# Four relations' count tables loaded as two plain halves and joined on VectorE

## The chip, the cores and the metric

The kernel runs on one core of one Trainium2 chip. The metric is device time in microseconds (us) of one execution; less is better. All arithmetic is in float32.

## The reference, cut to what matters

A graph network with two parts over the same 384 nodes: an attention layer (L0) and a two-layer relational convolution (L1) with 6 relations and 4 basis matrices. Only L1's use of the edge counts bears on the change:

```python
# one R-GCN convolution; n = 384 nodes, R = 6 relations, B = 4 bases, D = 768
W = jnp.einsum('rb,bio->rio', comp, basis)
h_all = jnp.einsum('ni,rio->rno', x, W)
counts = jnp.zeros((R, n), x.dtype).at[edge_type, dst].add(1.0)
norm = 1.0 / counts[edge_type, dst]
msg = h_all[edge_type, src] * norm[:, None]
agg = jax.ops.segment_sum(msg, dst, num_segments=n)
return agg + x @ root + bias
```

The sum over 12672 edges equals, for each relation r, a 384 x 384 matrix of edge counts, each column divided by its sum, times the nodes' features. The kernel works with these matrices.

## The kernel before, in words

**Counts.** Edges are scattered into tables in HBM: 99 indirect DMAs add counts into two tables of shape 6 x 384 x 384 (`put_count`, L269, issued by GpSimd, which the profile calls POOL). Two tables, `atab[0]` and `atab[1]`, are used in turn, so that one scatter needn't wait for the one just before it. The count of a relation is therefore the sum of two tables, `tabs[0][r]` and `tabs[1][r]`.

**Loading.** Tile `A` (128 partitions x 6 relations x 3 node blocks x 384) takes the counts. One relation of one table is 576 KB, in runs of 384 numbers. `tabs[1][r]` is loaded plainly (L834 for r = 0 and 1, L838 for the rest); `tabs[0][r]` is then added to it by the transfer itself, an accumulating DMA (`accum_op=ALU.add`, L836). All twelve DMAs are issued by POOL, in the order of the program.

**Shares.** `add_up(r)` (L339, L340) adds relation r's three node blocks on POOL into `sums[r]`. `share(r)` sums that over partitions with a matrix product by ones on TensorE (PE; L345, `ps_cnt`), makes max(count, 1) on ScalarE (ACT; L348, L349), its reciprocal on VectorE (DVE; L350) and scales `A[:, r]` with it (L351). `share(0)` and `share(1)` also call `add_up(4)` and `add_up(5)`.

**Mixing.** `mix(l, r, At)` accumulates comp[r, b] * A[:, r] into tile `At` (128 x 4 x 3 x 384, one slice for each basis b). For r = 0 ACT does it (L330), for the others DVE (L332). Before that, `At` serves as scratch: for transposed attention weights, and in the product with `w_in` for sums of weights (`S`). Its last readers there are matmuls of `ps_x`.

**The convolution's first layer** goes over four bases b = 0..3. For each, PE multiplies node blocks with weights in a first part of three steps c (L969) and in products of sums and differences (L963, a fast matrix multiplication scheme); ACT and DVE evacuate the results. DVE also makes the weights' differences for the next basis (`weight_sums`, L911 and L913) and, once the previous basis' last products are done, `last_sums` (L919). Those last products of a basis, `rest`, come after step c = 0 of the next. Weight tiles `w_c` come in on the SP queue as buffers come free. After the bases, the product with `root` (L1003), then the one with the mixed counts `At` (L1061).

**Order.** PE, POOL, SP and DVE (and ACT, from the attention on) follow a schedule written by hand: each engine executes in the order of the program text. The dictionary `between` says which piece of the share-and-mix work is put at which site; `go_between(l, b, c)` runs it after step c of basis b of layer l, and c = 4 is the end of a basis, after `weight_sums` for the next one. So an instruction of a share that waits on PE, DVE or POOL holds up all that stands behind it on that engine.

Of the kernel before, what the change touches and what calls it, by code (L numbers as in the profile page):

```python
# [15 lines left out]
ALU = mybir.AluOpType  # L16

P = 128
N = 384
NT = N // P  # L20
# [10 lines left out]
R = 6  # L31
# [11 lines left out]
MCELLS, ACELLS = N * N, N * R * N  # L43
# [8 lines left out]
def gnn_kernel(ctx: ExitStack, tc: tile.TileContext, out, x, edges, chunks, cols, rows, small,  # L52
               wq, wk, wv, wiq, wik, wiv, wo, w_in, basis, root, w_out):
    nc = tc.nc
# [15 lines left out]
    def next_bank(name, among=range(8)):  # L70

        i = next(i for i in ring if i in among)
        ring.remove(i)
        ring.append(i)
        return bank(i, name)
# [66 lines left out]
    def row_spread(st):  # L142

        mv = tiny.tile([P, 2], F32, tag="mv", name="mv")
        nc.vector.bn_aggr(mv, st.rearrange("p a b -> p (a b)"))
        sd = tiny.tile([P, 1], F32, tag="sd", name="sd")
        nc.vector.tensor_scalar(sd, mv[:, 1:2], LN_EPS, None, ALU.add)
        nc.scalar.activation(sd, sd, AF.Sqrt)
        return mv, sd
# [4 lines left out]
    def norm(t, h, mv, sd, parts=1):  # L154
        nc.vector.reciprocal(sd, sd)
        for cs in np.split(np.arange(D), parts):
            cs = slice(cs[0], cs[-1] + 1)
            nc.vector.tensor_scalar(h[:, cs], x_sb[:, t, cs], mv[:, 0:1], sd, ALU.subtract, ALU.mult)
# [14 lines left out]
    atab = [tables.tile([ACELLS + P, 1], F32, name=f"atab{i}") for i in range(2)]  # L173
# [149 lines left out]
    A = None  # L323

    def mix(l, r, At, bs=range(B)):

        for b in bs:
            w = small_sb[:, 4 + (l * R + r) * B + b:][:, :1]
            if r == 0:
                nc.scalar.activation(At[:, b], A[:, r], AF.Identity, scale=w)  # L330
            else:
                nc.vector.scalar_tensor_tensor(At[:, b], A[:, r], w, At[:, b], ALU.mult, ALU.add)  # L332
# [4 lines left out]
    def add_up(r):  # L337
        sums[r] = late.tile([P, N], F32, tag="sum", name="sum", bufs=4)
        nc.gpsimd.tensor_tensor(sums[r], A[:, r, 0, :], A[:, r, 1, :], ALU.add)  # L339
        nc.gpsimd.tensor_tensor(sums[r], sums[r], A[:, r, 2, :], ALU.add)  # L340

    def share(r):

        ps = next_bank("ps_cnt", [i for i in range(8) if i not in taken])
        nc.tensor.matmul(ps[:, :N], ones, sums[r], start=True, stop=True)  # L345
        rn = late.tile([P, N], F32, tag="rn", name="rn", bufs=2)

        nc.scalar.activation(rn, ps[:, :N], AF.Relu, bias=minus)  # L348
        nc.scalar.activation(rn, rn, AF.Identity, bias=ones[:, 0:1])  # L349
        nc.vector.reciprocal(rn, rn)  # L350
        nc.vector.tensor_tensor(A[:, r], A[:, r], rn[:, None, :].to_broadcast([P, NT, N]), ALU.mult)  # L351
        if r + 4 < R:
            add_up(r + 4)


    with ExitStack() as inner:
# [12 lines left out]
        def node_sum(T, i, X, dst):  # L369

            a, b = {1: (quarter(X, 0, 1), quarter(X, 0, 0)), 2: (quarter(X, 1, 1), T.get(1)),
                    3: (quarter(X, 1, 1), quarter(X, 0, 1)), 4: (quarter(X, 1, 0), T.get(2))}[i]
            nc.vector.tensor_tensor(dst, a, b, ALU.subtract)
            T[i] = dst
# [8 lines left out]
        def multiply(ps, a, b, start=False):  # L383

            for k in range(4):
                nc.tensor.matmul(ps, a[:, k, :], b[:, k, :], start=start and k == 0, stop=(k == 3),  # L386
                                 skip_group_check=not start)

        def open_banks(name):
            pb, pc, pa = [next_bank(name)[:, :HN] for _ in range(3)]  # L390
            return pa, pb, pc
# [33 lines left out]
        with tc.tile_pool(name="edge", bufs=1, side="right") as ep:  # L425
# [34 lines left out]
            def sum_tile(i):  # L460
                return ep.tile([P, 4, HN], F32, tag=f"T{i}", name="T")
# [21 lines left out]
            for n, (name, w, bias, part) in enumerate(plan):  # L483
# [33 lines left out]
                def rest(pa=pa, a=a, t=T[4], out=quads[1][0], b=bs[1], follow=follow if ends else None):  # L517
                    multiply(pa, a[1][1], t)
                    nc.scalar.activation(out, pa, AF.Identity, bias=b)
                    if follow is not None:  # L520
                        node_sum(T, 4, follow, sum_tile(4))
# [97 lines left out]
        At = late.tile([P, B, NT, N], F32, name="At")  # L619
        A = late.tile([P, R, NT, N], F32, tag="A", name="A")  # L620
# [207 lines left out]
                for t in range(2):  # L828
                    relu_T(h2T, t, xn[:, t, :], (0, 1), range(1, 8))
        norm(2, xn[:, 2, :], *row_spread(st[2]), parts=2)  # L830
        tabs = [tab[:ACELLS, :].rearrange("(t p r d) o -> r p t (d o)", p=P, r=R, t=NT) for tab in atab]

        for r in range(2):
            nc.gpsimd.dma_start(A[:, r], tabs[1][r])  # L834
        for r in range(R):
            nc.gpsimd.dma_start(A[:, r], tabs[0][r], accum_op=ALU.add)  # L836
            for n in {1: (2, 3), 2: (4,), 3: (5,)}.get(r, ()):
                nc.gpsimd.dma_start(A[:, n], tabs[1][n])  # L838
            if 0 < r < 5:
                add_up(r - 1)  # L840
        banks = [open_banks("ps_x") for _ in range(2)]

        def first_products(p):
# [41 lines left out]
                nc.scalar.activation(quad, pa, AF.Relu, bias=b)  # L885

        rest()


    with tc.tile_pool(name="conv", bufs=1) as cp:  # L890
# [38 lines left out]
        def shares(*rs):  # L929
            return lambda: [share(r) for r in rs]  # L930

        def mixes(l, r, *bs):
            return lambda: mix(l, r, At, bs)

        between = {(0, 2, 0): shares(0), (0, 2, 1): shares(1),
                   (0, 2, 2): shares(2), (0, 2, 4): lambda: [share(3), mix(0, 0, At)],
                   (0, 3, 0): shares(4), (0, 3, 1): shares(5),
                   (0, 3, 4): lambda: [mix(0, r, At) for r in range(1, R)],
                   (1, 0, 0): mixes(1, 0, 0, 1, 2, 3)}
# [305 lines left out]
```

## Time and profile before

| | |
|---|---|
| runs | 730.12, 732.62, 734.74 us, median 732.62 us |
| the profiled execution | 729.42 us, its span 727.6 us, mean granted clock of TensorE 0.99 |
| PE busy | 703.3 us (97%) |
| DVE busy | 515.2 us (71%) |
| POOL busy | 311.9 us (43%) |
| ACT busy | 157.6 us (22%) |
| DMA queue q0 (POOL's) | 9.60 MB, 11.2% of 16 engines' span |
| DMA queue q1 (SP's) | 78.44 MB, 30.5% |

The profile shows one execution. Times on its time axis count from the span's start. A group's line gives source line, engine, operation, tiles out<-in and shapes, how many, and busy time and mean; brackets or a last column tell how long the engine had been idle and what released it. The stage of interest lies between 407 us (the last scatter of counts) and 507 us (the last product of the first convolution layer begins).

### The profile page before, as it was taken

To read this page: it belongs to the slowest core of one execution; us is meant where nothing else is said; L and a number is where in the kernel's file an instruction comes from. 1 tells how busy PE (TensorE), PEld (TensorE's weight loads), DVE (VectorE), ACT (ScalarE), POOL (GpSimd) and SP (SyncE) were. 2 spreads that over 40 slices of the span, in tenths; PEclk is the share of its full clock that TensorE was granted. 3 is DMA by queue.
4 is the path that set the end of the run, shared out by engine and by line. 5 is a ranking of instruction groups with operands and counts; after the bars stand their busy time and mean duration, and the time that the engine had idled before them with its cause. 6 is when DMAs were issued, how large, how long until landed. Compare 5 with 4: busy or idle time off the path is not lost.

```text
span 727.6 us, 8832 instructions
## 1 busy us (share of the span) xinstructions
PE 703.3 (97%) x3228; PEld 528.8 (73%) x3228; DVE 515.2 (71%) x1307; ACT 157.6 (22%) x360; POOL 311.9 (43%) x239
## 2 busy tenths in 40 slices
PE   8999999999999999999999959999999999999995
PEld 7759999999996444488975535558975555579943
DVE  5886697969876799777444338899878676506756
ACT  3211111111112587300211115201131111011100
POOL 1366677778676688586785654100000000030000
PEclk9999999999999999999999989999999999999998
DMA  8786786274535522634324699221103213700001
GB/s 298 263 337 203 232 253 212 55 239 135 172 81 154 144 3 1 217 44 96 37 1 130 178 221 250 91 83 44 43 1 130 79 57 125 292 11 1 1 29 58
DMA packets 40024, 91.00 MB, mean 125 GB/s; under 512 B 19644, under 2 KB 26912, under 8 KB 35758
## 3 DMA queue, kind: packets, MB, share of 16 engines
q1 hardware_dynamic: 17678, 78.44, 30.5%
q0 software_dynamic: 21296, 9.60, 11.2%
q10 hardware_dynamic: 1008, 2.41, 0.9%
q8 instruction: 25, 0.41, 0.2%
q14 instruction: 17, 0.14, 0.1%
HBM read 79.27 MB, written 11.16 MB: 124 GB/s over the span
## 4 chain that ended last, share of the span: by engine, by line
PE 84%; DVE 9%; DMA 3%; ACT 2%; POOL 1%; issue 1%; SPq 0%; DVEq 0%; ACTq 0%
PE ps_g L969 11%; PE ps_k L386 10%; PE ps_c L1061 9%; PE ps_g L963 9%; PE ps_v L386 8%; PE ps_q L404 6%; PE ps_q L386 5%; PE ps_f L1167 4%; DVE At L332 4%; PE ps_y L386 3%; PE ps_c L1003 3%; PE ps_x L386 3%; DMA A<-atab 2%; PE ps_o L691 2%; PE ps_s L646 2%; PE ps_pT L680 2%
## 5 line engine op out<-in xcount | busy, mean ns | idle before, releaser
L269 POOL DMA_INDIRECT atab<-count,at x99 | 166.2, 1679 | 59.1 <-DMA atab<-count,at 32.2
L264 POOL DMA_INDIRECT mtab<-m_val,at x99 | 104.9, 1060 | 62.3 <-issue 25.2
L1154 POOL TENSOR_TENSOR x_sb<-x_sb,room 128x1024 f32<-128x1024 f32 x3 | 7.0, 2352 | 177.6 <-DMA room<-in_rows 177.6
L332 DVE SCALAR_TENSOR_TENSOR At<-A,small_sb,At 128x1152 f32<-128x1152 f32 x40 | 53.6, 1411 | 0.0
L969 PE MATMUL ps_g<-w_c,XT 128*128 128x384 f32 x144 | 49.2, 496 | 0.0
L963 PE MATMUL ps_g<-T,S 128*128 128x384 f32 x144 | 49.1, 486 | 0.0
L969 PE MATMUL ps_g<-w_c,XN 128*128 128x384 f32 x144 | 47.7, 487 | 1.1 <-DVE XN L1091 1.1
L404 PE MATMUL ps_q<-hT,w_q 128*128 128x384 f32 (+1 forms) x160 | 43.4, 436 | 1.4 <-DVE hT L97 1.4
L969 PEld LDWEIGHTS ps_g<-w_c,XT 128*128 128x128 f32 x144 | 28.1, 195 | 19.8 <-issue 1.8
L969 PEld LDWEIGHTS ps_g<-w_c,XN 128*128 128x128 f32 x144 | 27.3, 190 | 20.2 <-DVE XN L1091 1.4
L963 PEld LDWEIGHTS ps_g<-T,S 128*128 128x128 f32 x144 | 27.3, 190 | 19.2 <-ACT H L975 0.4
L404 PEld LDWEIGHTS ps_q<-hT,w_q 128*128 128x128 f32 x160 | 30.2, 200 | 14.1 <-ACT hT L90 1.7
L1061 PE MATMUL ps_c<-At,H 128*128 128x192 f32 x216 | 36.4, 326 | 0.0
L1061 PEld LDWEIGHTS ps_c<-At,H 128*128 128x128 f32 x216 | 35.4, 190 | 0.5
L386 PE MATMUL ps_k<-T,S 128*128 128x192 f32 x192 | 35.1, 326 | 0.0
L1091 DVE TENSOR_TENSOR XN<-XN,ps_c 128x192 f32<-128x192 f32 x38 | 12.5, 349 | 30.8 <-ACT XN L1047 19.7
L386 PEld LDWEIGHTS ps_k<-T,S 128*128 128x128 f32 x192 | 31.9, 190 | 0.0
L1167 PE MATMUL ps_f<-w_out,XN 128*128 128x512 f32 (+1 forms) x84 | 31.1, 531 | 0.0
L253 DVE SCALAR_TENSOR_TENSOR same<-keys,key,weigh 128x128 f32<-128x128 int32 x99 | 28.0, 348 | 0.9 <-DVE same L253 0.9
L659 DVE CUSTOM_DVE_ANT_0 s<-ps_s,mask 128x384 f32<-128x384 f32 x48 | 24.5, 549 | 5.2 <-PE ps_s L646 5.2
L253 DVE SCALAR_TENSOR_TENSOR same<-cells,own,later 128x128 f32<-128x128 int32 x99 | 27.9, 350 | 0.4
L1167 PEld LDWEIGHTS ps_f<-w_out,XN 128*128 128x128 f32 x84 | 15.9, 190 | 14.9 <-issue 14.3
(298 smaller groups left out, 1418.3 us busy)
## 6 DMA issues: line engine op xcount, KB each, us to landing
w_c<-in_basis SPq DMA_DIRECT2D x24, 768.0 KB
atab<-zero SPq DMA_DIRECT2D x12, 576.0 KB
A<-atab POOLq DMA_DIRECT2D x12, 576.0 KB
w_c<-in_root SPq DMA_DIRECT2D x6, 768.0 KB
w_q<-in_wq SPq DMA_DIRECT2D x4, 1024.0 KB
w_q<-in_wiq SPq DMA_DIRECT2D x4, 1024.0 KB
w_k<-in_wk SPq DMA_DIRECT2D x4, 1024.0 KB
w_k<-in_wik SPq DMA_DIRECT2D x4, 1024.0 KB
```

What stands on the lines that cost most here:

```text
L253: nc.vector.scalar_tensor_tensor(same, row[:, n, :], mine[:, c:c + 1], times, ALU.is_equal, ALU.mult, accum_out=count[:, i, c:c + 1])
L264: nc.gpsimd.indirect_dma_start(mtab[c // PER][:, :], bass.IndirectOffsetOnAxis(at[:, 0, c:c + 1], 0), m_val[:, c:c + 1], None)
L269: nc.gpsimd.indirect_dma_start(atab[0 if i < 11 else i % 2][:, :], bass.IndirectOffsetOnAxis(at[:, 1, c:c + 1], 0), count[:, 1, c:c + 1], ...
L332: nc.vector.scalar_tensor_tensor(At[:, b], A[:, r], w, At[:, b], ALU.mult, ALU.add)
L386: nc.tensor.matmul(ps, a[:, k, :], b[:, k, :], start=start and k == 0, stop=(k == 3), skip_group_check=not start)
L404: nc.tensor.matmul(ps[o][:, c], wt_[:, k, o * P:(o + 1) * P], src[:, k, c], start=(k == 0 and c.start == 0), stop=(k == KD - 1 and c.stop ...
L659: nc.vector.tensor_tensor_reduce(s[j], ps[:, :N], mask8[:, t, :], -scale, 3.0e38, ALU.add, ALU.min, tops[:, j:j + 1])
L963: nc.tensor.matmul(ps, x[:, c], y(c), start=start and c == 0, stop=(c == 2), skip_group_check=not start)
L969: nc.tensor.matmul(ps, block(XT, n, i)[:, c], w[c][:, i, o * HC:(o + 1) * HC], start=(first and c == 0), stop=(c == 2 and (i == 1 or ps is ...
L1003: nc.tensor.matmul(pr[o], w[k // 2][:, k % 2, o * P:(o + 1) * P], XT[:, k, :], start=(k == 0), stop=(k == KC - 1))
L1061: nc.tensor.matmul(ps, x[:, c], y[:, c], start=start and c == 0, stop=stop and c == 5, skip_group_check=True)
L1167: nc.tensor.matmul(p, XT[:, k, t * P:(t + 1) * P], w[k // 2][:, k % 2, c0:c1], start=(k == 0), stop=(k == KC - 1))
```

## The change

`tabs[0][r]` of relations 0 to 3 is no longer added by the transfer. It is loaded plainly into `At[:, r]`, which is free then, and a new function `join(r)` adds it to `A[:, r]` on DVE and then calls `add_up(r)`. Relations 4 and 5 keep the accumulating DMA. The DMAs' program text moves from ahead of the `w_in` products to behind them, and all of them are issued by POOL in one go: eight plain loads, then plain loads of relations 4 and 5, then their two accumulating DMAs. The calls of `add_up(0..3)` move from between the DMAs to the sites of the joins in `between`.

```diff
+    def join(r):
+
+        nc.vector.tensor_tensor(A[:, r], A[:, r], At[:, r], ALU.add)
+        add_up(r)
...
-        tabs = [tab[:ACELLS, :].rearrange("(t p r d) o -> r p t (d o)", p=P, r=R, t=NT) for tab in atab]
-
-        for r in range(2):
-            nc.gpsimd.dma_start(A[:, r], tabs[1][r])
-        for r in range(R):
-            nc.gpsimd.dma_start(A[:, r], tabs[0][r], accum_op=ALU.add)
-            for n in {1: (2, 3), 2: (4,), 3: (5,)}.get(r, ()):
-                nc.gpsimd.dma_start(A[:, n], tabs[1][n])
-            if 0 < r < 5:
-                add_up(r - 1)
         banks = [open_banks("ps_x") for _ in range(2)]
...
         rest()
+        tabs = [tab[:ACELLS, :].rearrange("(t p r d) o -> r p t (d o)", p=P, r=R, t=NT) for tab in atab]
+
+
+        for i, r in ((1, 0), (1, 1), (0, 0), (0, 1), (1, 2), (0, 2), (1, 3), (0, 3)):
+            nc.gpsimd.dma_start((A if i else At)[:, r], tabs[i][r])
+        for r in (4, 5):
+            nc.gpsimd.dma_start(A[:, r], tabs[1][r])
+        for r in (4, 5):
+            nc.gpsimd.dma_start(A[:, r], tabs[0][r], accum_op=ALU.add)
...
-        between = {(0, 2, 0): shares(0), (0, 2, 1): shares(1),
-                   (0, 2, 2): shares(2), (0, 2, 4): lambda: [share(3), mix(0, 0, At)],
+        between = {(0, 1, 4): lambda: join(0), (0, 2, 0): lambda: [join(1), share(0)],
+                   (0, 2, 1): lambda: [join(2), share(1)], (0, 2, 2): lambda: [join(3), share(2)], (0, 2, 4): lambda: [share(3), mix(0, 0, At)],
                    (0, 3, 0): shares(4), (0, 3, 1): shares(5),
                    (0, 3, 4): lambda: [mix(0, r, At) for r in range(1, R)],
```

## The prediction

> **What bounds the kernel now.** The page comes first: PE is busy for 97% of the span, so a change matters where PE idles, or where the chain of waits leaves PE. The list of waits on PE has one large entry, 7.3 us at `ps_cnt` L345 for POOL's sums, in the stage that the change touches. The timeline of PE there (start, us, group, idle before and releaser):
>
> ```profile
> 416.96 2.10 PE L963 MATMUL ps_g<-T,XT 128*128 128x384 f32 x6
> 425.32 1.65 PE L345 MATMUL ps_cnt<-sum,ones 128*128 128x384 f32 x2 [6.26 <-POOL sum L340]
> 426.76 5.34 PE L969 MATMUL ps_g<-w_c,XT 128*128 128x384 f32 x12
> 433.17 0.91 PE L345 MATMUL ps_cnt<-sum,ones 128*128 128x384 f32 x2 [1.07 <-POOL sum L340]
> 433.92 4.03 PE L969 MATMUL ps_g<-w_c,XT 128*128 128x384 f32 x12
> ```
>
> `share(0)` is wanted at 419.0 and runs at 425.3; `share(1)` waits 1.07 us more. What holds the sums is on POOL's timeline:
>
> ```profile
> 407.47 1.64 POOL L834 DMA_DIRECT2D A<-atab  x2 [0.23 <-PE ps_g L963]
> 412.41 1.31 POOL L836 DMA_DIRECT2D A<-atab  x1 [3.30 <-DMA A<-atab]
> 415.23 1.29 POOL L836 DMA_DIRECT2D A<-atab  x1 [1.51 <-issue]
> 416.01 2.12 POOL L838 DMA_DIRECT2D A<-atab  x2
> 423.21 0.99 POOL L339 TENSOR_TENSOR sum<-A 128x384 f32<-128x384 f32 x1 [5.08 <-DMA A<-atab]
> 424.27 0.99 POOL L340 TENSOR_TENSOR sum<-sum,A 128x384 f32<-128x384 f32 x1
> 427.92 1.30 POOL L836 DMA_DIRECT2D A<-atab  x1 [2.65 <-DMA A<-atab]
> 428.72 1.30 POOL L838 DMA_DIRECT2D A<-atab  x1
> 429.51 1.53 POOL L339 TENSOR_TENSOR sum<-A 128x384 f32<-128x384 f32 x1
> 431.12 2.00 POOL L340 TENSOR_TENSOR sum<-sum,A 128x384 f32<-128x384 f32 x1
> ```
>
> The reader is to see two things. POOL waits in its own order: the third L836 stood from 425.3 to 427.9 until relation 2's plain load had landed, and relation 1's sum behind it ran only then. And little has to land ahead of the first sum: two plain loads (the two L836 wait for them) and the accumulation of relation 0. Last, the DMA engines in windows (us; sum of the engines' busy times each; last column GB/s):
>
> ```profile
> 408.00:419.00 11.00, 11.00 (x35) 6.20 (x33) 5.39 (x8) 0.48 (x1) 5.31 (x6) 1.00 0.94 309
> 419.00:425.00 6.00, 0.06 (x1) 0.00 (x0) 1.50 (x3) 0.48 (x1) 1.72 (x2) 0.80 1.14 220
> 425.00:428.00 3.00, 2.68 (x4) 1.51 (x5) 0.00 (x0) 0.97 (x2) 0.35 (x2) 0.50 1.01 379
> ```
>
> The DMA share, last but one, is about 1 from 409 on: the engines are saturated. Accumulating transfers move 220 GB/s at a full share, plain ones 379. So an accumulation costs about 590 KB / 0.21 = 2.8 us of the engines' time and a plain load 590 / 0.39 = 1.5. From 468 on the chain is DVE's mixing (20 x 1.33 us, from 471.1), which starts when PE's last L963 product of basis 3 ends (470.64). PE's delay before that point passes whole to the end.
>
> **What the Trainium skill says.** "DMA: Bandwidth & Descriptors", section "Anatomy of one DMA — SWDGE (gpsimd) path": a DMA's semaphore wait is held on the issuing sequencer, the DMA engines only consume their queues. The trace agrees: 6.5 us in three waits of L836 on POOL. The same page, "Issuing engines are not separate DMA queues": whatever engine issues, transfers share the same 16 DMA engines. It agrees: from 412 to 414 us the window shows 0.50 MB of SP's queue and 0.24 of POOL's at full share. "TensorE: Matmul & The Clock Gate", section "What's actually happening": after about 3.4 us idle the clock is at half, and back after about as long of work. It agrees: idle from 418.9, clock 0.50 from 422.6 to 428.6. "SBUF — State Buffer", section "Who interferes with whom": a DVE operation on two SBUF inputs and a GpSimd one that reads SBUF exclude each other. It agrees: L340 took 2.00 us beside L351, 0.99 elsewhere.
>
> **The change part by part.**
>
> *Less DMA time.* Four accumulations become plain: 4 x (2.8 - 1.5) = 5.2 us of the engines' time less. The first of them no longer follows its own plain load. If nothing else were in the way, `share(0)` would need four loads and a join.
>
> *Joins on DVE.* Four additions of 128 x 1152 from SBUF, each as L351, 1.36 us. `join(0)` stands behind `weight_sums` for basis 2, which end at 418.2; it and `last_sums` behind it, and `join(1)`, run while PE waits: no cost. `join(2)` and `join(3)` stand behind `share(0)`'s and `share(1)`'s scaling, and put 2.7 us on DVE. DVE had 1.58 us idle before L984 at 468.8 and 1.31 before L986; with shares started later but PE behind them too, I find DVE still ahead there (below). Cost 0; without that cover at most 2.7.
>
> *Ten issues in a row on POOL, ahead of every sum.* This decides. In the changed program's order POOL issues eight plain loads, plain 4, plain 5, the accumulation of 4 (waits for plain 4's landing), that of 5 (waits for plain 5's), and only then `add_up(0)`. Before, `add_up(0)` needed two plain loads and one accumulation landed. Now it cannot start until the tenth plain load has landed, although its own data are there long before. The last scatter on POOL ends at 407.24 and the issues take 0.79 us each (L836 to L838, 415.23 to 416.01), so by 416 all ten plain loads are queued, and the DMA engines set the pace. Bytes ahead of the gate: 10 x 0.590 = 5.90 MB. SP's three `w_c` loads for basis 3, issued at 410.06, share the engines: 2.36 MB (in the trace they flow from 412 to 421). Together 8.26 MB. Data start at about 409.3. Rate: in 410 to 412, plain loads alone:
>
> ```profile
> q0 software_dynamic: 189, 0.80, 102.1%
> ```
>
> 0.80 MB in 2 us, 400 GB/s; in 412 to 416 with SP's transfers 380 to 390. At 390: 21.2 us, last byte at 430.5. Landing is seen up to 1.1 us after the last byte (relation 0: bytes done about 411.2, L836 at 412.4). So the accumulation of 5 issues at about 431.4. Its 1.30 us, then `add_up(0)` at 1.0 + 0.07 + 1.0 (DVE idle, no exclusion): **`share(0)` at 434.8 instead of 425.3, +9.5 us**.
>
> *What comes back.* `add_up(1)` follows at once, so `share(1)`'s 1.07 us wait and its longer product (0.91 for 0.65) go: -1.3. The half clock after the wait is paid in both (0.79 us of L345 and 1.5 of L969 beyond their usual times); a longer wait doesn't halve it again.
>
> *What is late next.* On POOL `add_up(4)` now stands before `add_up(2)`, and waits for the accumulation of 4: issued about 430, data from 432 at 0.2 MB/us, landed about 436; `add_up(1)` ends at 436.8. No wait. `add_up(2)` needs `join(2)`, behind `share(0)`'s reciprocal and scaling: 434.8 + 1.4 (product at half clock) + 1.2 (ACT) + 2.55 + 1.36 + 1.36 = 442.7, sum at 444.8. PE wants `share(2)` at 434.8 + 6.8 + 0.65 + 3.87 = 446.1. Margin 1.3 us; an exclusion with DVE (+1 us each) would use it up. `add_up(3)` at about 451 against 454.5. DVE then ends its scalings about 473, PE's L984 product about 476. Nothing more binds. The 0.66 us wait for ACT's L990 ahead of `share(4)` stays.
>
> Sum: +9.5 - 1.3 = **+8.2 us**, made against the profiled 729.42 (span 727.6 plus 1.8 around it): 737.6. The runs' median, 732.62, lies 3.2 above that profile; on its footing 740.8, I say 741.
>
> Unknown bounds. Rate of ten queued plain loads: 8.26 MB at 420 GB/s ends 1.5 us sooner; at 350, 2.4 later. If POOL's packets went wholly ahead of SP's, the gate would fall to 409.3 + 5.90/0.39 = 424.4 plus landing, 6 us sooner: +2. The trace has such loads shared, so I take the full 8.26. Side effects of deep queueing on POOL's issue: 0 to 3 us later, a gain is excluded since issue only adds.
>
> **Rivals.** (1) *A cheap gate*: SP's transfers get out of the way, or the rate is higher, +0 to +4 us, 733 to 737. For: from 410 to 412 only POOL's moved. Against: SP's bytes were at 0.3 to 0.4 MB/us from 414 to 418 while little of POOL's moved.
> (2) *A second wait*: `add_up(4)` ahead of `add_up(2)` stands for an accumulation that crawls. The second L836 took from 415.23 to about 425 to move its data. If that of 4 takes 10 us from a 431 issue plus a late landing, `share(2)` waits 2 to 5 us: total +11 to +14, 744 to 747. Against: SP's next loads come only at 443.8, so the queue is clear.
> (3) *Faster: POOL is not held.* If the loads drain before PE arrives, or the sums aren't behind the two waits, `join(0)` at 418.2 sets the time: `share(0)` at 418.2 + 1.36 + 2.1 + 0.1 = 421.8, -3.5, and -1.3 of `share(1)`: -4.8, 728. It decides where plain 5 lands before 418.5, that is over 640 GB/s for the POOL loads alone; 400 is the most seen. The change also does nothing else, so nothing of size can hide in another stage.
>
> **Chances.** The gate at the tenth load, +5 to +11: 0.68. Cheap gate 0.15, second wait 0.12, faster side 0.05. The range 734 to 748 holds the first, most of the second wait, and half of the cheap gate. One per cent, 7.3 us, is about what measuring this kernel can tell from no change; my likeliest case straddles it with its middle above, so slower by over 1% is 0.68 x 0.7 + 0.12 = 0.60, faster by over 1% 0.04 (the faster rival reaches only 0.7% unless its gain is larger), the rest, 0.36, within.
>
> **What would show it.** Right: on PE one wait of 14 to 17 us at `ps_cnt` for POOL's L340, with `share(0)` at 433 to 437 and no second one over 1 us; on POOL the accumulations idle until 429 to 433 for A<-atab, the first sum right behind; DVE's joins 0 and 1 finished some 8 us or more before it; POOL's queue at 390 GB/s with SP's until then. Wrong: the first sum before 427, or `share(2)` with a long wait, or DVE's mixing released by something other than PE's L963.

## The result, and the profile after

The changed kernel took 740.84 us (median; 734.19 to 742.07), the kernel before 732.39 us: ratio **1.0141, 95% interval 1.0099 to 1.0184**. Run again later (experiment 7), 1.0137 (1.0103 to 1.0172). It is slower by 1.4%, some 10 us. The profiled execution of it took 734.19 us (span 732.4), the lowest of its runs.

First PE's timeline of the changed kernel, in the stage whose lines were shown of before (start, us, group, idle before and its releaser):

```profile
413.48 2.10 PE L967 MATMUL ps_g<-T,XT 128*128 128x384 f32 x6
430.61 1.65 PE L350 MATMUL ps_cnt<-sum,ones 128*128 128x384 f32 x2 [15.03 <-POOL sum L340]
432.05 6.28 PE L973 MATMUL ps_g<-w_c,XT 128*128 128x384 f32 x12
438.17 0.81 PE L350 MATMUL ps_cnt<-sum,ones 128*128 128x384 f32 x2
```

One wait of 15.03 us at `share(0)`, where before showed 6.26 and 1.07; the second is gone. POOL's timeline tells why:

```profile
400.35 1.56 POOL L269 DMA_INDIRECT atab<-count,at  x1 [0.30 <-issue]
402.16 1.63 POOL L887 DMA_DIRECT2D A<-atab  x2 [0.26 <-PE ps_g L973]
...
409.29 1.57 POOL L889 DMA_DIRECT2D A<-atab  x2
425.68 1.31 POOL L891 DMA_DIRECT2D A<-atab  x1 [14.82 <-DMA A<-atab]
427.17 1.28 POOL L891 DMA_DIRECT2D A<-atab  x1 [0.19 <-issue]
427.97 1.51 POOL L339 TENSOR_TENSOR sum<-A 128x384 f32<-128x384 f32 x1
429.56 0.99 POOL L340 TENSOR_TENSOR sum<-sum,A 128x384 f32<-128x384 f32 x1
...
432.53 0.99 POOL L339 TENSOR_TENSOR sum<-A 128x384 f32<-128x384 f32 x1
433.60 1.00 POOL L340 TENSOR_TENSOR sum<-sum,A 128x384 f32<-128x384 f32 x1
438.92 1.00 POOL L339 TENSOR_TENSOR sum<-A 128x384 f32<-128x384 f32 x1 [4.32 <-DVE A L344]
```

All ten plain loads are issued by 410.9. Then POOL stands for 14.82 us at the first accumulating DMA (L891), which waits for relation 4's plain load; the trace's record of semaphores has that load landed at 425.4. The first sum comes right behind the second L891. DVE's timeline shows that the sum's data had been there long since:

```profile
414.65 0.96 DVE L915 TENSOR_TENSOR T<-w_c 128x768 f32<-128x768 f32 x1 [1.36 <-DMA w_c<-in_basis]
...
416.12 1.35 DVE L344 TENSOR_TENSOR A<-A,At 128x1152 f32<-128x1152 f32 x1
...
418.79 1.35 DVE L344 TENSOR_TENSOR A<-A,At 128x1152 f32<-128x1152 f32 x1
```

`join(0)` ended at 417.5, 10.5 us before its sum began. Transfers filled that time. Of the DMA engines, the two queues (packets, MB, share) between 418 and 420 us, SP's weights beside POOL's counts, and between 422 and 424 us, POOL's alone:

```profile
q1 hardware_dynamic: 80, 0.48, 61.1%
q0 software_dynamic: 81, 0.32, 41.2%
...
q0 software_dynamic: 178, 0.74, 102.4%
```

The two profiles don't start this stage at the same time: the last scatter on POOL ended at 407.24 before and at 401.91 after. So the difference of spans (4.8 us) isn't the change's price. PE waits at `share(0)` in both kernels, so the stage is measured from the end of that scatter to the DVE addition that releases the mixing. Before, its two ends are

```profile
405.69 1.55 POOL L269 DMA_INDIRECT atab<-count,at  x1 [0.30 <-issue]
470.66 0.55 DVE L986 TENSOR_TENSOR H<-H,ps_g 128x384 f32<-128x384 f32 x1 [1.31 <-PE ps_g L963]
```

and after, the second end is

```profile
475.34 0.55 DVE L990 TENSOR_TENSOR H<-H,ps_g 128x384 f32<-128x384 f32 x1 [1.31 <-PE ps_g L967]
```

It is 63.4 us before (407.24 to 470.66) and 73.4 after (401.91 to 475.34): **+10.0 us**. In the repeated profile it is 72.6 (407.76 to 480.40): +9.2. Both agree with the ratios. The scatter's end, 5.3 us sooner in the profile of after, takes +10.0 down to 4.7, the spans' 4.8. Counted from PE's arrival at `share(0)` instead (before 425.32 - 6.26 = 419.06, after 430.61 - 15.03 = 415.58), the stage takes 51.6 us before and 59.8 after, +8.2; that is less only because PE came 13.7 us after the scatter's end here and 11.8 us before, and a later arrival shortens the wait and nothing else.

For the experiments the first piece of the stage serves, from the end of the last scatter to `share(0)`. Before: 407.24 to 425.32, 18.1 us. After: 401.91 to 430.61, 28.7; in the repeated profile 407.76 to 435.97, 28.2.

### The profile page after: what moved, and what is told of

It reads as the page before. It is cut to its first block, busy times and chain, and to the rows that moved or that the text cites. A ratio compares the mean times of both kernels' runs of the same rounds, so it can differ in the third digit from the quotient of the medians.

```text
span 732.4 us, 8842 instructions
## 1 busy us (share of the span) xinstructions
PE 702.1 (96%) x3228; PEld 527.9 (72%) x3228; DVE 517.2 (71%) x1311; ACT 157.6 (22%) x360; POOL 303.8 (41%) x239
## 4 chain that ended last, share of the span: by engine, by line
PE 85%; DVE 8%; issue 3%; POOL 2%; ACT 1%; DMA 0%; DVEq 0%; ACTq 0%; POOLq 0%
PE ps_g L973 12%; PE ps_k L391 10%; PE ps_c L1065 9%; PE ps_g L967 9%; PE ps_v L391 8%; PE ps_q L409 6%; PE ps_q L391 5%; PE ps_f L1171 4%; DVE At L332 4%; PE ps_y L391 3%; PE ps_c L1007 3%; PE ps_s L651 3%; PE ps_x L391 3%; PE ps_o L696 3%; PE ps_pT L685 3%
## 5 line engine op out<-in xcount | busy, mean ns | idle before, releaser
L269 POOL DMA_INDIRECT atab<-count,at x99 | 163.2, 1648 | 58.8 <-DMA atab<-count,at 33.5
L973 PE MATMUL ps_g<-w_c,XT 128*128 128x384 f32 x144 | 50.2, 504 | 0.0
L973 PE MATMUL ps_g<-w_c,XN 128*128 128x384 f32 x144 | 47.7, 487 | 1.1 <-DVE XN L1095 1.1
L973 PEld LDWEIGHTS ps_g<-w_c,XT 128*128 128x128 f32 x144 | 28.5, 198 | 20.4 <-issue 2.7
L409 PE MATMUL ps_q<-hT,w_q 128*128 128x384 f32 (+1 forms) x160 | 41.8, 422 | 1.4 <-DVE hT L97 1.4
L973 PEld LDWEIGHTS ps_g<-w_c,XN 128*128 128x128 f32 x144 | 27.3, 190 | 20.2 <-DVE XN L1095 1.4
L409 PEld LDWEIGHTS ps_q<-hT,w_q 128*128 128x128 f32 x160 | 28.5, 190 | 14.1 <-ACT hT L90 1.7
L1095 DVE TENSOR_TENSOR XN<-XN,ps_c 128x192 f32<-128x192 f32 x38 | 12.5, 348 | 30.9 <-ACT XN L1051 19.7
## 6 DMA issues: line engine op xcount, KB each, us to landing
w_q<-in_wq SPq DMA_DIRECT2D x4, 1024.0 KB, 11.8
w_q<-in_wiq SPq DMA_DIRECT2D x4, 1024.0 KB, 13.6
```

The source lines that it names most:

```text
L269: nc.gpsimd.indirect_dma_start(atab[0 if i < 11 else i % 2][:, :], bass.IndirectOffsetOnAxis(at[:, 1, c:c + 1], 0), count[:, 1, c:c + 1], ...
L409: nc.tensor.matmul(ps[o][:, c], wt_[:, k, o * P:(o + 1) * P], src[:, k, c], start=(k == 0 and c.start == 0), stop=(k == KD - 1 and c.stop ...
L973: nc.tensor.matmul(ps, block(XT, n, i)[:, c], w[c][:, i, o * HC:(o + 1) * HC], start=(first and c == 0), stop=(c == 2 and (i == 1 or ps is ...
```

## The experiments

Ratios are against the kernel before on the same chip, with 95% intervals.

**1. All sums freed** (`e1_all_sums_free`). The accumulating DMAs go behind `add_up(1)`, the sums of 4 and 5 behind `add_up(3)`.

```diff
-        for r in (4, 5):
-            nc.gpsimd.dma_start(A[:, r], tabs[0][r], accum_op=ALU.add)
+        def accumulate():
+            for r in (4, 5):
+                nc.gpsimd.dma_start(A[:, r], tabs[0][r], accum_op=ALU.add)
...
-        if r + 4 < R:
-            add_up(r + 4)
...
-    (0, 2, 0): lambda: [join(1), share(0)],
+    (0, 2, 0): lambda: [join(1), accumulate(), share(0)],
...
-    (0, 2, 2): lambda: [join(3), share(2)],
+    (0, 2, 2): lambda: [join(3), add_up(4), add_up(5), share(2)],
```

> The two accumulating transfers are issued behind the sums of relations 0 and 1, and the sums of 4 and 5 behind those of 2 and 3; all else as in the changed kernel. Theory (POOL held by the two accumulations' waits ahead of every sum): share(0) runs when join(0) and its sum are done, so PE waits 3 to 5 us there instead of 15.0, and there is no second wait over 1 us; 729 to 731 us. Rival A (the data of relations 0 and 1 themselves come late, since ten loads and SP's weights fill the DMA engines): the wait stays 12 us or more, 738 to 742. Rival B (DVE's four joins are what costs): joins are as many and as long, so the time stays at 739 to 742 even if the wait at share(0) shrinks.

Measured: 0.9992 (0.9969 to 1.0016), so the whole loss is gone with all four joins still there: rival B falls. But the wait at `share(0)` was 8.99 us, not 3 to 5. DVE's timeline in this profile has the join

```profile
420.71 1.36 DVE L344 TENSOR_TENSOR A<-A,At 128x1152 f32<-128x1152 f32 x1 [5.82 <-DMA At<-atab]
```

and POOL's the sum of relation 0:

```profile
422.16 1.23 POOL L339 TENSOR_TENSOR sum<-A 128x384 f32<-128x384 f32 x1 [2.08 <-DVE A L344]
```

The sum now follows the join at once, and the join waits for data. Scatter's end (406.72) to `share(0)` (424.71) is 18.0 us, which is before's 18.1. The wait is long because PE came only 9.0 us after the scatter's end here (changed kernel: 13.7): 18.0 - 9.0 = 9.0. Relation 0's second half landed at 420.6, behind SP's three loads: SP had issued them at 406.73, just ahead of the counts, and from 410 to 412 the DMA engines moved 0.70 MB of SP's and 0.08 of POOL's. So rival A holds for the rest of the wait in this profile.

In the changed kernel's own profile SP's loads were issued 4.4 us after the first count load, and both halves of relation 0 had landed by 410.0; `join(0)` stood behind the weights' differences on DVE. It ended 15.6 us after the scatter, and its sum began 10.5 us later. So its 28.7 us are 18.2 us that stay without the gate, and 10.5 us of POOL being held. Whether plain loads and a join bring relation 0 sooner than plain loads and an accumulation can't be told: `share(0)` comes 16.3 to 18.5 us after the scatter with joins and POOL free (1, 2, 4, 6), and 18.1 and 19.7 with accumulations (before, 9).

**2. Only the issue moved** (`e2_only_issue_moved`): as 1, but `add_up(4)` and `add_up(5)` stay inside `share(0)` and `share(1)`.

> Only the two accumulating transfers are moved behind the sums of relations 0 and 1; the sum of 4 still stands ahead of that of 2. Theory: share(0) waits 3 to 5 us, but the sum of 4 now waits for an accumulation that is issued when the last plain load has landed, and holds the sum of 2: a second wait of 4 to 7 us at share(2); 735 to 738 us. Rival A: first wait 12 us or more, 738 to 742. If the order of the sums doesn't matter: no second wait, 729 to 731.

Measured: 1.0121 (1.0074 to 1.0167), hardly better than the changed kernel; about 9 us above before, where 3 to 6 were expected. PE's timeline:

```profile
424.67 1.65 PE L350 MATMUL ps_cnt<-sum,ones 128*128 128x384 f32 x2 [8.21 <-POOL sum L340]
...
442.06 1.65 PE L350 MATMUL ps_cnt<-sum,ones 128*128 128x384 f32 x2 [6.43 <-POOL sum L340]
```

The first wait is of the size that relation 0's own data cost in 1 (8.99). (In this profile the first load into `At` was itself held for 4.08 us, by the profile for DVE; in the changed kernel it wasn't, and `share(0)` comes no later after the scatter for it, 16.3 us.) The second is new, and POOL's timeline shows the sum of 4, ahead of that of 2, waiting for the accumulation of 4 to land:

```profile
436.78 1.15 POOL L339 TENSOR_TENSOR sum<-A 128x384 f32<-128x384 f32 x1 [3.60 <-DMA A<-atab]
```

The two waits add up to 14.6 us, about the changed kernel's 15.0, and after each the product runs at half clock (1.65 us for 0.81). The gate had only moved to the next instruction of POOL that waits for a late transfer.

**3. Relations 4 and 5 first in the queue** (`e3_4_and_5_first`): the plain loads of 4 and 5 are issued ahead of the other eight; the accumulating DMAs stay ahead of all sums.

> The plain loads of relations 4 and 5 go first in the queue instead of last; the accumulations stay ahead of all sums on POOL. Theory: the accumulations' waits end with an early load (about 12 us after the first issue), so they hold no sum; share(0) waits 4 to 6 us, a little longer than with the queue's old order because its data come two loads later; the accumulated data come last in the queue, so the sum of 4 holds that of 2 for 2 to 5 us; 732 to 737 us. Rival A (late data): relation 0's data come two loads later still, share(0) waits 16 to 18 us, 741 to 744.

Measured: 1.0049 (1.0026 to 1.0073), that is 736 on before's first median and inside the expected span. The first wait was 9.81 us, longer than expected; that at `share(2)` 0.22, shorter. POOL's timeline:

```profile
421.03 1.31 POOL L891 DMA_DIRECT2D A<-atab  x1 [3.26 <-DMA A<-atab]
424.50 1.28 POOL L891 DMA_DIRECT2D A<-atab  x1 [2.16 <-DMA A<-atab]
```

The two L891 began 11.0 and 14.5 us after the first issue (410.03) instead of 23.5 and 25.0, though their place among POOL's instructions was the same. So the gate is the landing of what they wait for, not the accumulating DMA as such. But here they did not wait for the plain loads of 4 and 5, which by the semaphores had landed at 414.5 and 416.0. In all these programs POOL's DMAs report their landing on eight semaphores in turn, and a DMA also waits for the one eight places before it. The accumulations are the eleventh and twelfth DMA, and waited for the third and fourth load, landed at 420.7 and 424.2. In the changed kernel this turn cost nothing: its third and fourth load had landed by 413.5, those of 4 and 5 at 425.4 and 426.9, right before the two L891. Scatter to `share(0)` is 21.1 us: 3 more than in 1, for two loads more ahead of relation 0.

**4. No accumulation at all** (`e4_no_accumulation`): as 1, with `tabs[0][4]` and `[5]` loaded plainly into `At[:, 0]` and `At[:, 1]` once joined, and two more joins behind `join(3)`.

> As the first experiment, but relations 4 and 5 are joined on DVE too: their second halves are loaded plainly into the two slices of At that join(0) and join(1) have read. No accumulating transfer is left. Theory (joins lie beside other work, POOL is free): 728.5 to 731 us, within 1 us of the first experiment. Rival B (DVE's joins cost what they take): two more joins, 2.7 us, show in full: 2 to 3 us above the first experiment.

Measured: 0.9989 (0.9968 to 1.0011), the same as 1 within 0.03%: two more joins cost nothing that shows. DVE's idle time ahead of L988 in basis 3 fell from 3.00 us in 1 to 0.61. A further join of 1.35 us would then show by some 0.7 us, by these figures; it wasn't tried.

**5. The kernel before with its sums last** (`e5_before_sums_last`): no join, no load into `At`; only the place of the sums.

```diff
-            if 0 < r < 5:
-                add_up(r - 1)
+        for r in range(4):
+            add_up(r)
```

> The kernel before, with one edit: the sums of relations 0 to 3 stand behind all twelve transfers on POOL, as in the changed kernel. No join, no second set of plain loads. Theory (the place of the sums behind the last two accumulations' waits is the cost, not joins or plain loads): share(0) waits until plain 5 has landed behind three more accumulations, 15 to 19 us later than before; the time goes up by 13 to 18 us. Rival B (joins on DVE or loads into At cost): the edit alone costs under 3 us.

Measured: 1.029 (1.0247 to 1.0334), 18 to 24 us; more than the 13 to 18 expected, and clearly not under 3. In POOL's timeline the last two accumulations are each held by a plain load that lands behind earlier accumulations, and then comes the first sum:

```profile
434.31 1.31 POOL L836 DMA_DIRECT2D A<-atab  x1 [7.61 <-DMA A<-atab]
438.61 1.30 POOL L836 DMA_DIRECT2D A<-atab  x1 [2.99 <-DMA A<-atab]
439.41 1.53 POOL L339 TENSOR_TENSOR sum<-A 128x384 f32<-128x384 f32 x1
```

From the first load's issue (406.19) to `share(0)` (442.06) it is 35.9 us, before 17.9: 18.0 later, inside the 15 to 19 expected. So the order on POOL alone makes such a loss. Why the time grew by more stays open. In this profile POOL's first load was itself held for 5.16 us by a weight transfer, and PE waited 7.4 us in the k and v projections (before 1.3); whether the other runs had this isn't known.

**6. Shares one site later** (`e6_sites_late`): as 1, but `share(0)` at (0, 2, 1), and so on to `share(5)` at (0, 3, 2); `join(2)` ahead of the accumulations.

> As the first experiment (sums free), with every share put one site later, so that PE has one more step c of products ahead of share(0), and the two accumulations behind the sum of relation 2. Theory: what is left of the wait at share(0), 9.0 us in the first experiment's profile, is the data's own arrival; 3.9 us more PE work ahead of it cuts the wait by that; DVE still ends its scalings in time. 1.5 to 5.5 us below the kernel before. Rival: DVE's scalings, now later, hold the mixing, and nothing is won: within 1 us of the kernel before.

Measured: 0.9953 (0.9928 to 0.9978), 3.4 us below before. The wait at `share(0)` is 0.97 us, but not all of the difference from 1's 8.99 is gain: PE reached the old site 13.7 us after the scatter's end here, and 9.0 us in 1. From the scatter's end to the addition that releases the mixing it is 57.7 us, in 1 61.5: 3.8 less. A part of the rival has come true as well: DVE has no idle time from 426.8 to 466.1, where its mixing starts. It costs little so far, as PE's last product ahead of it ended at 464.8 and the addition began at 465.67.

**7. The changed kernel again** (`e7_changed_again`).

> The changed kernel again, unaltered, on the chip of these runs: 6 to 11 us above the kernel before, share(0) 27 to 30 us after the last scatter on POOL has ended.

Measured: 1.0137 (1.0103 to 1.0172), +10.0 us; scatter to `share(0)` 28.2 us; both as expected.

**8. More traffic on SP's queue** (`e8_more_traffic`): two loads of 1.18 MB into `spare` behind the weights of basis 3, parts 0 and 1.

> The changed kernel with two more plain loads on SP's queue (1.18 MB each, into a tile that nothing reads any more), issued right behind the weight loads that run beside the count loads. Theory (the gate is bytes ahead of it on shared, saturated DMA engines): 1.2 to 2.4 MB more ahead of the last count load at 0.39 MB/us put share(0) 3 to 6 us later, 31 to 35 us after the last scatter; 3 to 6 us above the changed kernel. Rival (POOL's own queue has a rate of its own, or its packets go first): under 1 us.

Measured: 1.0152 (1.0104 to 1.0201), not told apart from 7. Inconclusive: SP issued the loads at 419.8 in the profile, after POOL's first L891 (419.42), so they couldn't delay the gate. The profile shows something else. PE had come to this stage late, after waits of 8.7 us in the k and v projections (before 1.3); it reached `share(0)` at 427.1 and waited 3.08 us, and the sum was released by `join(0)`. The gate had opened, at 421, before PE came. So what the gate costs differs from one execution to the next: only the part by which POOL is later than PE counts.

**9. The kernel before with late sites** (`e9_before_sites_late`): accumulations as before, the sites of 6, and `add_up(1)` ahead of the third L836.

> The kernel before, accumulating transfers and all, with two edits of order: every share one site later, as in the sixth experiment, and the sum of relation 1 ahead of the third accumulation's wait. No join. If the late sites alone made the sixth experiment's gain: 2 to 6 us below the kernel before, as good as the sixth experiment or better, since DVE has four joins (5.4 us) less. If the plain loads and joins are what made it: within 1 us of the kernel before.

Measured: 0.9946 (0.9905 to 0.9988), as good as 6. So 6's gain needs no plain loads and no joins; they add nothing that can be seen. The late sites and the earlier sum of relation 1 weren't tried apart. This and 6 are faster than both kernels, by some 0.5% than the kernel before.

**10. More traffic on ACT's queue** (`e10_more_traffic_act`):

```diff
+        def more_traffic():
+            nc.scalar.dma_start(spare.rearrange("p i k n -> p (i k n)"),
+                                w_in[0].rearrange("p k n -> p (k n)")[:, :2304])
...
-        between = {(0, 1, 4): lambda: join(0),
+        between = {(0, 1, 4): lambda: [more_traffic(), join(0)],
```

> The changed kernel with one more plain load of 1.18 MB into a tile that nothing reads any more, issued on ACT's queue at the end of basis 1, while the count loads run. Theory (bytes on shared, saturated engines set the gate): 1.18 / 0.39 = 3.0 us more from the first count load's issue to the last accumulation's, which was 25.0 and 24.6 us in the two profiles of the changed kernel: 27 to 28.5. Rival (POOL's queue has a rate of its own or goes first): 24.5 to 25.5.

Measured: 1.0197 (1.0157 to 1.0236). POOL's timeline:

```profile
408.85 1.64 POOL L887 DMA_DIRECT2D A<-atab  x2 [0.22 <-issue]
...
434.75 1.31 POOL L891 DMA_DIRECT2D A<-atab  x1 [14.07 <-DMA A<-atab]
436.29 1.28 POOL L891 DMA_DIRECT2D A<-atab  x1 [0.23 <-issue]
```

27.4 us from first to last issue, against 25.0 and 24.6 in the two profiles of the changed kernel (and 23.7 in 8's, whose added traffic came too late to count): 2.4 to 3.7 us more for 1.18 MB, and the wait on PE is 20.36 us. Bytes of another queue move the gate at 0.32 to 0.49 MB/us, which is about the engines' rate. In this run POOL's transfers neither went first nor had a rate of their own. The tenth load was issued only at 419.93, held for 3.04 us by the turn of eight semaphores; the engines were at full share meanwhile (1.02 from 416 to 420).

## Why the prediction was right, point by point

| step of the prediction | forecast | measured |
|---|---|---|
| first load's issue to the accumulation of 5 | 431.4 - 407.47 = 23.9 us | 25.0 and 24.6 us |
| last scatter to `share(0)` | 27.6 us | 28.7 and 28.2 us (before 18.1) |
| `share(1)`'s wait and longer product go | -1.3 us | gone, 1.07 and 0.1 us |
| no wait at `share(2)`; margin | 1.3 us | sum at 440.98, product at 442.68: 1.7 us |
| accumulation of 4 landed before `add_up(4)` | no wait, 0.8 us to spare | no wait at 432.53; landed at 432.2 |
| joins on DVE | 0 (at most 2.7) | 0: PE still late for DVE's L988, by 3.75 us |
| change of the stage, from the scatter's end | +8.2 us | +10.0 and +9.2 us |
| time | 741 us | 740.84 us |

- **The gate** is as argued: experiment 1 takes the sums from behind it and the loss is gone; 5 puts before's sums behind one and makes a loss; 3 moves its landing; 10 moves it by bytes.
- **Its size** was forecast 1 to 2 us too small: +8.2 us, and +10.0 and +9.2 measured. The gate opened about 1 us later after the scatter than forecast, since the engines moved 0.375 MB/us over those 22 us (8.26 MB, 404 to 426) instead of 0.39. And the prediction put PE's half clock at the same cost in both kernels; but the twelve L973 took 6.28 us (5.98 in the repeated profile) for 5.34.
- **That 741 met 740.84 is partly luck.** The ratio's interval goes from 7 to 13.5 us, so it holds +8.2 without singling it out, and the medians happen to differ by 8.45.
- **A count was too high.** The prediction says that `share(0)` would need four loads and a join. It needs relation 0's two halves, the first and the third load of the queue (in 1, `join(0)` began right after the third landed, at 420.6). The gate's sum doesn't use this count.
- **A label was wrong.** SP's three loads beside the counts aren't all basis 3's: with five buffers the first is basis 2's third part. The trace of the change shows it, as DVE's third L915 waits 1.36 us for `w_c`. The bytes were right. That wait lies under PE's 15 us.
- **The rival "a cheap gate"** fails on the split of the engines: 0.43 to 0.49 MB of SP's beside 0.31 to 0.37 of POOL's in each 2 us from 410 to 420. **"A second wait"** doesn't occur in the changed kernel, but it is real where the first is taken away (experiment 2). **"POOL is not held"** fails, and experiment 1 adds that its price was too hopeful: without the gate `share(0)` comes 18.0 us after the scatter there, not the 14.6 (421.8 - 407.24) of that rival, because relation 0's second half lands later than DVE is ready. In the changed kernel's profile its data were in time, but DVE itself was late: `join(0)` began 14.2 us after the scatter, where that rival has 11.0.

## What to carry to other kernels

POOL issues DMAs in order and also computes here, and its computation stood behind every DMA that waited for a semaphore (14.82 us at one). Before batching transfers "in one go" on such an engine, list for each instruction which landing stands ahead of it; the turn of semaphores can add a wait that the data don't ask for (experiment 3). Moving one such instruction may only uncover the next (experiment 2), so move all that wait for late data. Where PE waits for data that can't come sooner, giving PE other work first (experiments 6 and 9) was worth more here than making the data's transfer cheaper: 0.5% against nothing that shows (experiment 1).

## What was not expected of the hardware

Four accumulations less brought the first sum no measurable gain, although an accumulation costs the engines about 2.8 us and a plain load 1.5. The time from the scatter to `share(0)` spreads over 16.3 to 19.7 us (before, 1, 2, 4, 6, 9), whichever kind brings the data. One thing that moves the data's arrival is when SP's loads are issued: in experiment 1 they ran ahead of the counts, and relation 0's second half landed 13.9 us after the scatter, against 8.1 us in the changed kernel. No run tests this alone.

The clock of PE after a wait. A window of before (the clock is the last column but two):

```profile
428.60:432.00 3.40, 3.40 (x10) 1.71 (x8) 3.31 (x2) 0.00 (x0) 3.32 (x4) 0.89 0.55 81
```

and of the changed kernel:

```profile
430.60:434.00 3.40, 3.39 (x6) 1.88 (x7) 0.45 (x1) 1.20 (x2) 3.24 (x4) 0.50 1.16 202
434.00:436.00 2.00, 2.00 (x5) 1.09 (x4) 2.00 (x1) 0.00 (x0) 0.60 (x1) 0.50 0.21 35
436.00:438.20 2.20, 2.20 (x8) 1.23 (x7) 2.10 (x3) 0.00 (x0) 0.00 (x0) 0.87 0.00 0
```

In the traces' record of the clock it is full again at 429.4 in before (the prediction's 428.6 is the end of a window that it asked for) and at 436.6 in the changed kernel, 4.1 and 6.0 us after work began; over all runs with a wait of 5 us or more at `share(0)` it takes 3.0 to 6.0 us. The length of the wait doesn't order them: after 20.36 us (experiment 10) and after 8.99 (experiment 1) it is 3.0 us each. But the whole stretch at half clock is 6.9, 10.2, 13.6, 17.1 or 20.4 us, each time a multiple of 3.4. "TensorE: Matmul & The Clock Gate", section "What's actually happening", in the Trainium skill, has a window of about 3.4 us that runs freely, whatever the kernel does. The traces agree with that, though the switch comes over a wider range than the half microsecond either way that the page gives. How long PE works at half clock then depends on where in the window its wait happens to end, which a forecast can't place.
